# Row blocks woven by two and by four, and an image kept in place, beside a chain of selective scans

## The chip, the cores and the metric

The kernel runs on one core of a Trainium2 chip. What counts is the time of one execution on the device, in microseconds (us). A core has five engines with instruction queues of their own: TensorE (PE; the loading of its weights is shown apart as PEld), VectorE (DVE), ScalarE (ACT), GpSimd (POOL) and SyncE (SP). Here SP issues nearly all DMA transfers, in the order in which they were written down. Each engine takes its instructions strictly in order; an instruction that waits holds up all behind it on the same engine.

## The reference

The input is a batch of four images, each with 96 channels of 64 x 64 pixels (L = 4096). Four layers follow one another, each as x = x + layer(group_norm(x)):

- layer 0: attention of the pixels on pooled queries, and a look at neighbours, then a 5 x 5 depthwise convolution of the values and a projection;
- layer 1: a selective state space layer (`in` projection, 3 x 3 depthwise convolution, scans in four directions over the image, layer norm, a gate), then a block of 1 x 1 (c1), 3 x 3 depthwise (c2) and 1 x 1 (c3) convolutions and a squeeze-and-excitation gate;
- layer 2: a 3 x 3 sharpening filter;
- layer 3: a 1 x 1 convolution with ReLU, a linear layer, and two depthwise branches from it. `x1 = silu(conv(h, dw1))` goes through another selective state space layer. `x2 = silu(conv(h, dw2))` is gated:

```python
x2 = jax.nn.silu(conv2d(h, dw2_w, dw2_b, groups=C))
g = jax.nn.sigmoid(conv2d(jax.nn.relu(conv2d(x2, ag1_w, ag1_b)), ag2_w, ag2_b))
y = x1 + x2 * g
```

The heart of both state space layers is a recurrence along the pixels, `h = h * exp(delta * A) + delta * u * B`, `y = sum over 16 states of h * C`, for 192 channels, 16 states and four directions. For one image and layer these are 12,288 rows of 4096 pixels, or 96 tiles of 128 rows in four chunks of 1024 pixels: 384 units, and eight times that for four images and two layers.

## The kernel before, in words

`streams` (L901) holds everything. Its main loop goes through 3072 units, 384 for each of eight scans (`SCANS`: layer 1 of images 0 and 1, layer 3 of 0 and 1, then the same for 2 and 3). One unit handles 128 rows over a chunk of 1024 pixels:

- SP fetches the step sizes `rep`, four units ahead (L2038);
- ACT takes the exponential, two units ahead (`decays`, L2046), and copies the state at the chunk's end (`carry_on`, L2074);
- PE spreads the inputs into a PSUM tile `bx` (`drive`, two ahead, two such tiles);
- DVE multiplies `bx` by B, one unit ahead (`times_b`, L2059), and runs the recurrence (`scan`, L2066);
- POOL multiplies the result by C (`times_c`, L2078);
- every fourth unit, PE sums states into `acc` (`collect`, 16 matmuls), two to five units behind.

All matmuls have one line, L1028 (`mm`); all weights that are not kept throughout are loaded by `staged` (L991, the transfer named `arena<-in_w`).

Beside the scans runs a generator of side work: `first` (layer 0 and layer 1's `in_conv`), `second` (the rest of layer 1, layer 2, and layer 3 up to its scan), `third` and `last` (the end of layer 3, through `finish`). While scan s goes, `beside(s)` brings other images forward: phases 0, 3 and 4 do `first` of images 1 to 3, phases 1, 2, 5 and 6 `second` of images 0 to 3, and phase 7 `third` three times and `last`. `first` of image 0 runs alone at the start ("the head", to 661 us), and the rest of `last` alone at the end.

The order is written out by hand. A unit gives the side work up to three slots (`Slots.begin` and `end`) against a budget per unit, `PACE`. In the generator, `yield` alone ends the issue of matmuls, whose results the rest of the slot reads; a number ends a step and costs at least half of it; a tuple marks one tap of a convolution, of which as many are taken as the budget holds; `WAIT` uses up the unit's budget. Whatever the generator issues goes into the engines' queues between the scan's own instructions. The preparation of the next group of scans (`prepare`) takes part of most units in the same manner.

PSUM for the side work is two banks, handed out in turn by `bank()`. A step that asks for a bank waits until the last reader of the tile that had it is done. SBUF for the side work is one `arena`, in which `Stack` pools lie on top of each other; a new tile waits for the last users of the bytes under it.

The places that the change touches, by the lines of the kernel before:

- `attention`: keys and queries, a block of 512 pixels at a time: matmul, copy on ACT, square on ACT (L1327), matmul with the heads' ones, maximum on DVE (L1332);
- `first`: weights `l0_*` are staged inside `attention` and again before the 5 x 5 taps; `mix` is the loop of taps, sum, projection and sum (L1491 and L1497); `l1_in` is staged after the second group norm (L1505), right before `in_conv`;
- `second`: c1, c2 and c3 over nine row steps; the squeeze-and-excitation gate (L1619 to L1622); then the residual image is loaded from `res1`, added (L1630), stored to `res1`, loaded once more into a new tile `X`, and normed (L1166 is the norm's first pass on ACT). The norm of layer 3, the 1 x 1 convolution and linear layer (`line`, L1659 and L1664), the gate (L1675 SiLU, L1681 ReLU, L1687 Tanh, L1688 product), x1 (L1699) and `in_conv`;
- `finish`: the gate of the state space layer, SiLU (L1818) and product (L1819).

The gate's rows in `second` are done one after the other, and the last two lines stand in one step:

```python
nc.scalar.activation(q[:96], q[:96], AF.Tanh, bias=half_ag2, scale=0.5)
nc.vector.scalar_tensor_tensor(out=x2, in0=q[:96], scalar=1.0, in1=x2, op0=ALU.add, op1=ALU.mult)
```

Of the kernel before, what the change touches and what calls it, by code (L numbers as in the profile page):

```python
# [9 lines left out]
F32 = mybir.dt.float32  # L10
# [890 lines left out]
def streams(ctx: ExitStack, tc: tile.TileContext, x, wts, cst, out, wat, cat, flag):  # L901
# [42 lines left out]
    class Stack:  # L944
# [14 lines left out]
        def tile(self, shape, dtype, name, tag=None, bufs=None):  # L959
            n = int(np.prod(shape[1:]))  # L960
            tag = tag or name
            if tag not in self.slots:
# [5 lines left out]
                if shape[0] > 96:  # L968
                    self.dirty += [(a, n) for a in self.slots[tag]]
            a = self.slots[tag].pop(0)  # L970
            self.slots[tag].append(a)
            v = arena[: shape[0], a : a + n]
# [252 lines left out]
    def in_conv(pool, tag, b, w, src):  # L1225
# [3 lines left out]
        for h in range(2):  # L1229
# [7 lines left out]
            uc = pool.tile([96, W, H], F32, name="uc", bufs=1)  # L1237
# [69 lines left out]
    def attention(b, xn, samp, dist):  # L1307

        with Stack(2) as pool:
            w = staged(pool, "l0_k", "l0_q", "l0_v")  # L1310
# [14 lines left out]
            def squares(p, o):  # L1325
                sq = pool.tile([96, PCH], F32, tag="sq", name="sq", bufs=1)
# [8 lines left out]
            for j in range(8):  # L1335
                p = bank()
                mm(p[:96], w["l0_k"], xn[:, bass.ts(j, PCH)])
                yield
                nc.scalar.copy(kk[:, bass.ts(j, PCH)], p[:96])
                yield from squares(p[:96], top[:, 0, j : j + 1])  # L1340
            for j in range(2):
# [6 lines left out]
                yield from squares(p[:96], top[:, 1, j : j + 1])  # L1348
            two = small.tile([96, 2], F32, name="two")
# [6 lines left out]
            for pair in [((0, e), (1, e)) for e in range(4)] + [((2, 0), (2, 1)), ((2, 2), (2, 3))]:  # L1356
# [22 lines left out]
                rs = pool.tile([64, Q], F32, tag="sq", name="rs", bufs=1)  # L1379
# [63 lines left out]
    def first(b):  # L1443

        with Stack(1) as P:
            xn = P.tile([96, L], F32, name="xn")
            for j in range(4):
                nc.sync.dma_start(out=xn[:, bass.ts(j, CH)], in_=x[b][:, bass.ts(j, CH)])
            yield from group_norm(xn, img(xn))
            with Stack(1) as D:  # L1450
# [13 lines left out]
                yield from attention(b, xn, samp, dist)  # L1464
                with Stack(1) as FP:
                    feat = FP.tile([96, L], F32, name="feat")
                    yield from neighbours(b, xn, samp, dist, feat)
                    with Stack(1) as pool:
                        w = staged(pool, "l0_v", "l0_proj")
# [11 lines left out]
                        for j in range(8):  # L1481
# [19 lines left out]
            yield from group_norm(xn, img(xn))  # L1501
            for j in range(4):
                nc.sync.dma_start(out=gate1[b][:, bass.ts(j, CH)], in_=xn[:, bass.ts(j, CH)])
            with Stack(1) as pool:
                w = staged(pool, "l1_in")["l1_in"]  # L1505
                yield from in_conv(pool, "l1_", b, w, xn)

    def directions(pool, b, tag):

        V = pool.tile([96, 2, L], F32, name="V", bufs=1)  # L1510
# [29 lines left out]
        return V  # L1540

    def second(b):

        with Stack(1) as PX:
            V = yield from directions(PX, b, "l1_")
# [17 lines left out]
            with Stack(2) as pool:  # L1563
                w = staged(pool, "l1_c1", "l1_c3", "l1_se2")
# [6 lines left out]
                sums = pool.tile([96, 8], F32, name="sums", bufs=1)  # L1571
                for j in range(9):
                    here, last = band[j % 2], band[(j - 1) % 2]
                    if j < 8:
                        for q in range(4):
# [6 lines left out]
                            yield 2  # L1582
                    if j == 0:
# [39 lines left out]
                X = V[:, 1, :]  # L1623
                for j in range(4):
                    nc.sync.dma_start(out=X[:, bass.ts(j, CH)], in_=res1[b][:, bass.ts(j, CH)])
                for j in range(8):
                    js = bass.ts(j, PCH)
                    p = bank()
                    nc.scalar.activation(p[:96], V[:, 0, js], AF.Copy, scale=s2)
                    nc.vector.tensor_add(X[:, js], X[:, js], p[:96])  # L1630
                    nc.sync.dma_start(out=res1[b][:, js], in_=X[:, js])
                    yield 1
        with Stack(1) as R2:
            hp = R2.tile([96, PADW, PADW], F32, name="hp")
            border(hp, 1)
            with Stack(2) as pool:
                X = pool.tile([96, L], F32, name="X", bufs=1)
                for j in range(4):
                    nc.sync.dma_start(out=X[:, bass.ts(j, CH)], in_=res1[b][:, bass.ts(j, CH)])
# [13 lines left out]
                for j in range(8):  # L1653
                    js = bass.ts(j, PCH)
                    p = bank()
                    mm(p[:96], w["l3_c1"], X[:, js])
# [642 lines left out]
```

## Time and profile before

| | |
|---|---|
| time, median of three runs | 13,912.74 us (13,892.47 to 13,918.34) |
| the profiled execution's own time | 13,902.53 us |
| its span, first to last instruction | 13,900.7 us |
| mean granted TensorE clock | 0.899 |
| the scan's loop | 661 to 13,781 us |
| phases begin at | 661, 2268, 3888, 5480, 7080, 8670, 10,258 and 11,848 us |

The page gives, for each engine, its busy time, and below that groups of instructions: line, engine, operation, output <- input, shape and count, then the total of busy time, the mean of one in ns, and the idle time of the engine before them with what ended most of it. "Waits" list for each engine what its instructions waited for: total us, times, and the longest. In a timeline a line is one instruction or several alike: start, duration, engine, line, operation, and in brackets the idle time before it and the releaser. A releaser is worked out from semaphore events, and a matmul's end is modelled, so that a busy PE may still have been slow.

### The profile page before, as it was taken

To read this page: it belongs to the slowest core of one execution; us is meant where nothing else is said; L and a number is where in the kernel's file an instruction comes from. 1 tells how busy PE (TensorE), PEld (TensorE's weight loads), DVE (VectorE), ACT (ScalarE), POOL (GpSimd) and SP (SyncE) were. 2 spreads that over 40 slices of the span, in tenths; PEclk is the share of its full clock that TensorE was granted. 3 is DMA by queue.
4 is the path that set the end of the run, shared out by engine and by line. 5 is a ranking of instruction groups with operands and counts; after the bars stand their busy time and mean duration, and the time that the engine had idled before them with its cause. 6 is when DMAs were issued, how large, how long until landed. Compare 5 with 4: busy or idle time off the path is not lost. (4 is left out here: it accounts for less than half of the span.)

```text
span 13900.7 us, 127815 instructions
## 1 busy us (share of the span) xinstructions
PE 11053.6 (80%) x40137; PEld 3344.3 (24%) x40802; DVE 11634.9 (84%) x7509; ACT 8696.5 (63%) x12314; POOL 10284.9 (74%) x4730
## 2 busy tenths in 40 slices
PE   8878886988779796878868887897969887677756
PEld 3322221322223221222212221232313222111111
DVE  1478988987989888889888898898989988877886
ACT  3366576666756676665766566666856677665654
POOL 1177887877878777788878888787878878666674
PEclk9999998998889897999979998998979998888867
DMA  0267888887878888778877788787888878767774
GB/s 11 64 170 198 202 221 214 204 212 183 230 196 219 212 211 214 187 193 213 221 194 197 196 209 230 192 222 196 224 212 207 222 198 229 183 176 195 184 201 115
DMA packets 846672, 2695.23 MB, mean 194 GB/s; under 512 B 112480, under 2 KB 115008, under 8 KB 845984
## 3 DMA queue, kind: packets, MB, share of 16 engines
q1 hardware_dynamic: 845328, 2685.08, 75.7%
q8 instruction: 324, 5.31, 0.2%
q14 instruction: 364, 2.98, 0.1%
q10 hardware_dynamic: 656, 1.87, 0.0%
HBM read 2186.34 MB, written 500.17 MB: 193 GB/s over the span
## 5 line engine op out<-in xcount | busy, mean ns | idle before, releaser
L2078 POOL TENSOR_TENSOR rep<-hs,bc 128x1024 f32<-128x1024 f32 x3072 | 7226.5, 2359 | 2578.9 <-DVE hs L2066 2189.7
L1028 PE MATMUL one<-arena 128*96 128x512 f32 (+5 forms) x11072 | 5273.9, 602 | 699.8 <-ACT arena L1375 138.0
L2066 DVE TENSOR_TENSOR_SCAN hs<-rep,carry,bx 128x1024 f32<-128x1024 f32 x2304 | 5401.6, 2344 | 296.7 <-ACT carry L2074 25.6
L2059 DVE TENSOR_TENSOR bx<-bx,bc 128x1024 f32<-128x1024 f32 x3072 | 3717.8, 1210 | 666.5 <-PE bx L1028 485.7
L2046 ACT ACTIVATE rep<-rep,l_decay 128x1024 f32<-128x1024 f32 x3072 | 3496.9, 1143 | 799.0 <-DMA rep<-dd 782.4
L1028 PE MATMUL bx<-parts,spread 128*128 128x512 bf16 x5479 | 1879.2, 418 | 1322.8 <-DVE hs L2066 1199.8
L1028 PEld LDWEIGHTS one<-arena 128*96 128x96 f32 (+4 forms) x11072 | 1791.7, 172 | 3128.9 <-issue 1800.3
L2066 DVE TENSOR_TENSOR_SCAN hs<-rep,bx 128x1024 f32<-128x1024 f32 x768 | 1754.4, 2284 | 133.7 <-ACT carry L2074 53.5
L1028 PE MATMUL acc<-rep,ct 128*32 128x512 f32 x12288 | 1712.5, 670 | 12.9 <-POOL rep L2078 9.7
L1028 PEld LDWEIGHTS <-spread 128*128 128x128 bf16 x6144 | 444.6, 100 | 3633.6 <-DVE hs L2066 2362.8
L1028 PE MATMUL one<-pr,ct 64*96 64x512 f32 x1024 | 629.7, 699 | 92.4 <-ACT pr L1953 37.2
L1375 ACT ACTIVATE arena<-one 128x512 f32<-128x512 f32 x576 | 342.3, 595 | 489.8 <-PE one L1028 488.3
L1028 PEld LDWEIGHTS acc<-rep,ct 128*32 128x32 f32 x12288 | 359.1, 118 | 1163.5 <-issue 935.6
L2046 ACT ACT_TABLE_LOAD x482 | 618.4, 1283 | 8.5
L2074 ACT COPY carry<-hs 128x1 f32<-128x1 f32 x2304 | 408.3, 177 | 233.0 <-DVE hs L2066 231.5
L1028 PE MATMUL bx<-arena 128*96 128x512 f32 (+5 forms) x1120 | 489.2, 576 | 34.8 <-DMA arena<-in_w 16.7
L1028 PE MATMUL one<-arena,ct 128*96 128x512 f32 x508 | 294.0, 687 | 249.9 <-ACT arena L1526 177.0
L1028 PE MATMUL held<-arena,cols 128*32 128x256 f32 x3072 | 479.4, 394 | 13.4 <-ACT arena L1375 11.7
L1028 PE MATMUL held<-arena 128*32 128x256 f32 x3072 | 479.9, 394 | 0.0
L982 POOL MEMSET arena<- 32x1024 f32 (+5 forms) x81 | 54.1, 691 | 403.8 <-ACT arena L1375 331.5
L1028 PE MATMUL one<-us,wt 128*38 128x512 f32 x1024 | 284.6, 677 | 72.9 <-DMA us<-urow 36.0
L1988 ACT ACT_TABLE_LOAD x256 | 328.4, 1283 | 4.4
(3322 smaller groups left out, 9857.3 us busy)
## 6 DMA issues: line engine op xcount, KB each, us to landing
rep<-dd SPq DMA_DIRECT2D x3072, 512.0 KB
parts<-du SPq DMA_DIRECT2D x1024, 144.0 KB
bc<-rows SPq DMA_DIRECT2D x256, 512.0 KB
dd<-delta SPq DMA_DIRECT2D x256, 384.0 KB
du<-cut SPq DMA_DIRECT2D x256, 384.0 KB
yrow<-yo SPq DMA_DIRECT2D x128, 512.0 KB
ycol<-yo SPq DMA_DIRECT2D x128, 512.0 KB
us<-urow SPq DMA_DIRECT2D x128, 384.0 KB
```

What stands on the lines that cost most here:

```text
L982: nc.gpsimd.memset(arena[96:, k : min(k + CH, a + n)], 0.0)
L1028: nc.tensor.matmul(o, lhsT=lhsT, rhs=rhs, start=first, stop=last)
L1375: nc.scalar.activation(last.rearrange("p a b -> p (a b)"), p, AF.Exp, scale=HD**-0.5)
L1988: nc.scalar.activation(w, w, AF.Ln)
L2046: nc.scalar.activation(a, a, AF.Exp, scale=decay[tag][:, k, NG * h + m : NG * h + m + 1])
L2059: nc.vector.tensor_mul(bx, bx, ready[i // NG][2][:, 0, :])
L2066: nc.vector.tensor_tensor_scan(out=hs, data0=a, data1=bx, initial=carry[:, h, m : m + 1] if c else 0.0, op0=ALU.mult, op1=ALU.add)
L2074: nc.scalar.copy(carry[:, h, m : m + 1], live[i][1][:, CH - 1 : CH])
L2078: nc.gpsimd.tensor_tensor(a, hs, ready[i // NG][2][:, 1, :], ALU.mult)
```

## The change

A helper `weave(made, depth)` goes round a list of generators; in each pass it takes in one more while fewer than `depth` are active, and runs each up to its next number. Keys and queries, mix and line are passed through it with depth 2, the gate's rows (`skip`) with depth 4. In the gate a step of 0.5 is put between Tanh and product, x2 has five buffers and g1 three, both sets of diagonals are built at the start, and one unit's budget is given up after that. `sq` has four buffers (shared with `ex`) instead of one.

In `second` the residual image X is the second half of V for the rest of the stage. It is loaded from `res1` in row step 7 of c1/c2, and not stored there again; copy and sum of the residual become two half steps. x1 and the turned image of `in_conv` lie in V too.

Weights are staged elsewhere: layer 0's at the start of `first`, `l1_in` ahead of the second group norm, c1, c3 and se2 at the start of `second`; `l3_in` right ahead of `in_conv` instead of ahead of x1's convolutions. In `finish`, a step of 0.5 lies between the gate's SiLU and its product.

```diff
@@ -1222,7 +1222,7 @@
-    def in_conv(pool, tag, b, w, src):
+    def in_conv(pool, tag, b, w, src, turned=None):
@@ -1234,7 +1234,7 @@
                 yield 1
-            uc = pool.tile([96, W, H], F32, name="uc", bufs=1)
+            uc = turned if turned is not None else pool.tile([96, W, H], F32, name="uc", bufs=1)
             for j in range(8):
@@ -1304,10 +1304,26 @@
-    def attention(b, xn, samp, dist):
+    def weave(made, depth):
+
+        left, active = list(made), []
+        while left or active:
+            if left and len(active) < depth:
+                active.append(left.pop(0))
+            for g in list(active):
+                while True:
+                    try:
+                        v = next(g)
+                    except StopIteration:
+                        active.remove(g)
+                        break
+                    yield v
+                    if v is not None and not isinstance(v, tuple):
+                        break
+
+    def attention(b, xn, w, samp, dist):
         with Stack(2) as pool:
-            w = staged(pool, "l0_k", "l0_q", "l0_v")
             kk = pool.tile([96, L], F32, name="kk", bufs=1)
@@ -1332,13 +1348,14 @@
-            for j in range(8):
+            def keys(j):
                 p = bank()
...
                 yield from squares(p[:96], top[:, 0, j : j + 1])
-            for j in range(2):
+
+            def queries(j):
                 p = bank()
@@ -1346,6 +1363,8 @@
                 yield from squares(p[:96], top[:, 1, j : j + 1])
+
+            yield from weave([keys(j) for j in range(8)] + [queries(j) for j in range(2)], 2)
             two = small.tile([96, 2], F32, name="two")
@@ -1446,6 +1465,7 @@
                 nc.sync.dma_start(out=xn[:, bass.ts(j, CH)], in_=x[b][:, bass.ts(j, CH)])
+            w = staged(P, "l0_v", "l0_k", "l0_q", "l0_proj")
             yield from group_norm(xn, img(xn))
@@ -1461,12 +1481,11 @@
                 yield 2
-                yield from attention(b, xn, samp, dist)
+                yield from attention(b, xn, w, samp, dist)
                 with Stack(1) as FP:
...
                     with Stack(1) as pool:
-                        w = staged(pool, "l0_v", "l0_proj")
                         vpad = pool.tile([96, 68, 68], F32, name="vpad")
@@ -1478,7 +1497,7 @@
                             nc.sync.dma_start(out=xn[:, bass.ts(j, CH)], in_=x[b][:, bass.ts(j, CH)])
-                        for j in range(8):
+                        def mix(j):
                             js = bass.ts(j, PCH)
@@ -1498,16 +1517,17 @@
                             yield 1
-            yield from group_norm(xn, img(xn))
-            for j in range(4):
-                nc.sync.dma_start(out=gate1[b][:, bass.ts(j, CH)], in_=xn[:, bass.ts(j, CH)])
+
+                        yield from weave([mix(j) for j in range(8)], 2)
             with Stack(1) as pool:
                 w = staged(pool, "l1_in")["l1_in"]
+                yield from group_norm(xn, img(xn))
+                for j in range(4):
+                    nc.sync.dma_start(out=gate1[b][:, bass.ts(j, CH)], in_=xn[:, bass.ts(j, CH)])
                 yield from in_conv(pool, "l1_", b, w, xn)
-    def directions(pool, b, tag):
-
-        V = pool.tile([96, 2, L], F32, name="V", bufs=1)
+    def directions(V, b, tag):
+
         with Stack(1) as T:
@@ -1537,12 +1557,14 @@
                 yield 1
-        return V
...
         with Stack(1) as PX:
-            V = yield from directions(PX, b, "l1_")
+            V = PX.tile([96, 2, L], F32, name="V", bufs=1)
+            held_w = Stack(1).__enter__()
+            w = staged(held_w, "l1_c1", "l1_c3", "l1_se2")
+            yield from directions(V, b, "l1_")
             with Stack(2) as pool:
@@ -1561,7 +1583,6 @@
             with Stack(2) as pool:
-                w = staged(pool, "l1_c1", "l1_c3", "l1_se2")
                 dg = [diagonals(pool, wv("l1_c2")[:, q, :], f"dg{q}") for q in range(4)]
@@ -1569,6 +1590,7 @@
                 sums = pool.tile([96, 8], F32, name="sums", bufs=1)
+                X = V[:, 1, :]
                 for j in range(9):
@@ -1580,6 +1602,9 @@
                             yield 2
+                    if j == 7:
+                        for k in range(4):
+                            nc.sync.dma_start(out=X[:, bass.ts(k, CH)], in_=res1[b][:, bass.ts(k, CH)])
                     if j == 0:
@@ -1620,23 +1645,17 @@
                 nc.vector.tensor_scalar(s2, s2, 1.0, None, ALU.add)
-                X = V[:, 1, :]
-                for j in range(4):
-                    nc.sync.dma_start(out=X[:, bass.ts(j, CH)], in_=res1[b][:, bass.ts(j, CH)])
                 for j in range(8):
...
                     nc.scalar.activation(p[:96], V[:, 0, js], AF.Copy, scale=s2)
+                    yield 0.5
                     nc.vector.tensor_add(X[:, js], X[:, js], p[:96])
-                    nc.sync.dma_start(out=res1[b][:, js], in_=X[:, js])
-                    yield 1
-        with Stack(1) as R2:
-            hp = R2.tile([96, PADW, PADW], F32, name="hp")
+                    yield 0.5
+            held_w.__exit__()
+            hp = PX.tile([96, PADW, PADW], F32, name="hp")
             border(hp, 1)
             with Stack(2) as pool:
-                X = pool.tile([96, L], F32, name="X", bufs=1)
-                for j in range(4):
-                    nc.sync.dma_start(out=X[:, bass.ts(j, CH)], in_=res1[b][:, bass.ts(j, CH)])
                 pad = pool.tile([96, PADW, PADW], F32, name="pad2", bufs=1)
@@ -1650,10 +1669,10 @@
                 yield from group_norm(X, img(X))
-                for j in range(8):
-                    js = bass.ts(j, PCH)
+
+                def line(j):
                     p = bank()
-                    mm(p[:96], w["l3_c1"], X[:, js])
+                    mm(p[:96], w["l3_c1"], X[:, bass.ts(j, PCH)])
                     yield
@@ -1663,21 +1682,25 @@
                     yield 1
+
+                yield from weave([line(j) for j in range(8)], 2)
             with Stack(2) as pool:
...
                 dg = diagonals(pool, wv("l3_dw2_w"))
-                for j in range(8):
-                    js = bass.ts(j, PCH)
+                dg1 = diagonals(pool, wv("l3_dw1_w"), "diag1")
+                yield WAIT
+
+                def skip(j):
                     p = bank()
                     yield from conv(p[:96], dg, hp, j)
-                    x2 = pool.tile([96, PCH], F32, name="x2")
+                    x2 = pool.tile([96, PCH], F32, name="x2", bufs=5)
                     nc.scalar.activation(x2, p[:96], AF.Silu, bias=wv("l3_dw2_b"))
...
                     yield
-                    g1 = pool.tile([48, PCH], F32, name="g1")
+                    g1 = pool.tile([48, PCH], F32, name="g1", bufs=3)
                     nc.scalar.activation(g1, p[:48], AF.Relu, bias=wv("l3_ag1_b", 48))
@@ -1685,21 +1708,23 @@
                     nc.scalar.activation(q[:96], q[:96], AF.Tanh, bias=half_ag2, scale=0.5)
+                    yield 0.5
                     nc.vector.scalar_tensor_tensor(out=x2, in0=q[:96], scalar=1.0, in1=x2, op0=ALU.add, op1=ALU.mult)
-                    nc.sync.dma_start(out=skip3[b][:, js], in_=x2)
+                    nc.sync.dma_start(out=skip3[b][:, bass.ts(j, PCH)], in_=x2)
                     yield 1
-            with Stack(1) as pool:
-                x1 = pool.tile([96, L], F32, name="x1", bufs=1)
-                dg = diagonals(pool, wv("l3_dw1_w"))
-                w = staged(pool, "l3_in")["l3_in"]
+
+                yield from weave([skip(j) for j in range(8)], 4)
+                x1 = V[:, 0, :]
                 for j in range(8):
...
                     p = bank()
-                    yield from conv(p[:96], dg, hp, j)
+                    yield from conv(p[:96], dg1, hp, j)
                     nc.scalar.activation(x1[:, js], p[:96], AF.Silu, bias=wv("l3_dw1_b"))
...
                     yield 1
-                yield from in_conv(pool, "l3_", b, w, x1)
+            with Stack(1) as pool:
+                w = staged(pool, "l3_in")["l3_in"]
+                yield from in_conv(pool, "l3_", b, w, x1, V[:, 1, :].rearrange("p (a b) -> p a b", b=H))
@@ -1715,7 +1740,8 @@
         with Stack(1) as PX:
-            V = yield from directions(PX, b, "l3_")
+            V = PX.tile([96, 2, L], F32, name="V", bufs=1)
+            yield from directions(V, b, "l3_")
             yield from finish(PX, b, V, [(0, range(8))])
@@ -1816,6 +1842,7 @@
                         nc.scalar.activation(p[:96], p[:96], AF.Silu)
+                        yield 0.5
                         nc.vector.scalar_tensor_tensor(out=V[:, h, js], in0=V[:, h, js],
```

Not shown: the list of regions that a pool clears holds each only once and takes in every tile over 96 partitions; a name or two in signatures.

More of the change, by code (lines that the diff above doesn't have):

```diff
@@ L967, in tile @@
                 assert mark[0] <= ARENA, mark[0]
-                if shape[0] > 96:
-                    self.dirty += [(a, n) for a in self.slots[tag]]
             a = self.slots[tag].pop(0)
             self.slots[tag].append(a)
+            if shape[0] > 96 and (a, n) not in self.dirty:
+                self.dirty.append((a, n))
             v = arena[: shape[0], a : a + n]
@@ L1325, in squares @@
             def squares(p, o):
-                sq = pool.tile([96, PCH], F32, tag="sq", name="sq", bufs=1)
+                sq = pool.tile([96, PCH], F32, tag="ex", name="sq", bufs=4)
                 nc.scalar.activation(sq, p, AF.Square)
@@ L1378, in attention @@
                 yield
-                rs = pool.tile([64, Q], F32, tag="sq", name="rs", bufs=1)
+                rs = pool.tile([64, Q], F32, name="rs", bufs=1)
                 nc.vector.reciprocal(rs, av[:64, :Q])
```

## The prediction

> **What bounds the kernel now.** I read the page's busy shares first, then the groups of the scan's line, then the windows of one phase, and last the waits of DVE, PE and ACT over the loop (661 to 13,781 us).
>
> The page, span and busy shares:
>
> ```profile
> span 13900.7 us, 127815 instructions
> PE 11053.6 (80%) x40137; PEld 3344.3 (24%) x40802; DVE 11634.9 (84%) x7509; ACT 8696.5 (63%) x12314; POOL 10284.9 (74%) x4730
> ...
> L2066 DVE TENSOR_TENSOR_SCAN hs<-rep,carry,bx 128x1024 f32<-128x1024 f32 x2304 | 5401.6, 2344 | 296.7 <-ACT carry L2074 25.6
> L2059 DVE TENSOR_TENSOR bx<-bx,bc 128x1024 f32<-128x1024 f32 x3072 | 3717.8, 1210 | 666.5 <-PE bx L1028 485.7
> ```
>
> DVE is the fullest engine, and it sets the time as a chain: each of 3072 units does one scan (2.34 us) and one product (1.21 us). By the scans' start times a unit with nothing else on DVE takes 3.60 us. 3072 of these are 11,060 us; the loop takes 13,119 us. Some 2,060 us are therefore excess, which the side work causes: DVE instructions of its own, or waits that it puts in DVE's queue or ahead of PE's `bx` matmuls. Only that can change. The side work of all phases but the eighth is done 30 to 47 units before its phase ends, so that spreading it over more units costs nothing by itself.
>
> Waits of DVE in the loop (total us, times, longest):
>
> ```profile
> DVE bx L2059 <- PE bx L1028: 485.7, 263, 17.2
> DVE arena L1688 <- ACT one L1687: 94.2, 30, 5.8
> ...
> DVE arena L1332 <- PE one L1028: 48.2, 21, 4.5
> ...
> DVE arena L1819 <- ACT one L1818: 33.6, 29, 2.7
> ...
> DVE arena L1630 <- DMA arena<-res: 11.9, 5, 7.9
> ```
>
> The second line is layer 3's gate: the product with the tanh (L1688) stands at once behind Tanh's order, and Tanh behind a matmul; a scan queued behind it waits too. The first collects what holds PE up; PE's and ACT's own waits say what:
>
> ```profile
> PE one L1028 <- DMA arena<-in_w: 67.4, 12, 10.4
> ...
> PE one L1028 <- ACT arena L1681: 39.3, 30, 3.1
> ```
>
> ```profile
> ACT arena L1166 <- DMA arena<-res: 32.8, 3, 11.3
> ...
> ACT arena L1166 <- DMA arena<-in_w: 12.3, 1, 12.3
> ```
>
> A matmul waits up to 10.4 us for staged weights, with the `bx` matmuls queued behind it; ACT waits four times, 45.1 us, for the image that `second` has just stored and loads again (the fourth is filed under in_w, but its line reads that image).
>
> **The change part by part.** All against the profiled execution: span 13,900.7 plus 1.8 around it, 13,902.5 us. It is 10.2 below the median of 13,912.7, inside the runs' 13,892 to 13,918.
>
> *1. Weave by two (keys and queries, mix, line): 0.* `weave` adds one generator per pass and each row yields a number twice. So row 1 begins only after row 0's second number: the issue order stays k0, h0, k1, h1. In the changed program's instruction streams the order is the same as before on PE up to the second stage's pooled vectors, and on DVE through all of phase 0. `sq` with four buffers instead of one moves nothing while the order stays. L1332's 48.2 us remain.
>
> *2. Layer 3's gate by four: -84.* Rows have four numbers now, so here the order does change: the convolution of row j+1 and the other rows' steps come between Tanh and product, and the product follows by a round. By the scans, the 32 units that hold the gate's rows take 155.4, 153.8, 149.8 and 148.6 us in the four images; quiet they would take 115.3. Excess together 146.4. Of it stays DVE's own 32 products x 0.686 = 22; the neighbouring stage (x1's eight convolutions, no waits) has an excess of 3.5 in 24 units, 0.15 per unit, so 34 units x 4 = 20; and PE still waits for ReLU (L1681 39.3, here only as far as no row lies between): I leave 20. 146 - 62 = 84. Bounds: 50 if the ReLU and SiLU waits (39.3 and L1675's 28.8, about half on the path) come on top; 124 if only the products stay. PE is a ceiling near: 130 us busy in such a stretch of 150.
>
> ```profile
> 9606.00:9756.00 150.00, 129.48 (x391) 39.01 (x398) 116.23 (x72) 102.41 (x140) 100.59 (x44) 0.93 0.68 171
> ...
> 3391.00:3485.00 94.00, 91.77 (x302) 31.23 (x306) 87.24 (x52) 72.02 (x82) 79.34 (x35) 0.99 0.83 221
> ```
>
> These windows (length; PE, PEld, DVE, ACT, POOL busy; clock; DMA) show the gate's stretch and x1's: there PE is 98% busy, and DVE still goes at 3.7 us per unit. The second set of diagonals puts two POOL instructions of 1.63 us back to back ahead of `times_c`; POOL is 100 of 150 busy there, and `collect` stands two units behind: 0.
>
> *3. The image in place: -39.* Gone are eight stores and four loads per image and the waits for them: at the norm's start the units have an excess of 13.4, 8.7, 8.1 and 8.5 = 38.7. The read of `res1` moves to row 7 of c1/c2: its last part waits on SP for PE's last reader, and the `rep` loads queued behind it run four units (14 us) ahead, so it is hidden; without that cover it would cost one c1 step, about 5. Bounds -43 and -30.
>
> *4. Residual: -8.* L1630 no longer waits for the image (11.9). Its copy and sum are split by a half slot; the sum may come later, never earlier. Bounds 0 and -18.
>
> *5. Weights earlier.* `l1_in` before the norm: PE gaps of 9.5, 10.4, 10.4 and excesses of 6.0, 8.3, 8.4 in these units (three images; the first's is in the head), against 1.9 where the same convolution starts without a wait: -17 (-10 to -23). Layer 0's weights and c1's at their stage's start: PE gaps of 8.3, 7.4, 7.8 and 1.5, 3.3, 3.3, and 5.5 where layer 2's weights stood in SP's queue behind the image's loads, 37 in all. `l1_in`'s gaps cost 17 of 30; these are shorter, and two `bx` buffers cover more of a short one, so I take 40%: -15 (-30 to 0). In the head the first value matmul at 40.3 waits 16.7 for weights, while `xn` is ready at 32.9: -7 (-8 to -3).
>
> *6. `l3_in` later: +23.* Today it is staged 24 convolutions before its use; now at the start of `in_conv`, with the first matmul in the same slot. Nearest row, the same form for `l1_in`:
>
> ```profile
> 1878.32 0.43 SPq L991 DMA_DIRECT2D arena<-in_w  x1
> ...
> 1883.23 1.99 PE L1028 MATMUL one<-arena 128*96 128x512 f32 x2 [9.51 <-DMA arena<-in_w]
> ...
> 1886.12 1.23 DVE L2059 TENSOR_TENSOR bx<-bx,bc 128x1024 f32<-128x1024 f32 x1 [5.88 <-PE bx L1028]
> ```
>
> Issue to matmul is 4.91 us; on PE it costs 9.51 because SP's order, the drive of the next unit and DVE all stand behind. 4 x (7.6 - 1.9) = +23; bounds +15 and +34.
>
> *7. Gates of the finish: 0 (-20 to +31).* A half slot between SiLU (L1818) and product (L1819). The same generator goes on, so no other side work comes between, and DVE's order stays; the next unit's Exp can come between. That makes 24 more table loads on ACT (14 for SiLU, 10 for Exp):
>
> ```profile
> 12007.66 1.28 ACT L2046 ACT_TABLE_LOAD   x1
> 12008.96 1.15 ACT L2046 ACTIVATE rep<-rep,l_decay 128x1024 f32<-128x1024 f32 x1
> ```
>
> 24 x 1.28 = 31 us of an ACT that is 63% busy, beside DVE; on the path at worst all of it. Against that stand 33.6 us that L1819 waits now, of which some may go.
>
> This is where a rule speaks against the change. The Trainium skill (ScalarE: Activation LUTs, "What ACT_TABLE_LOAD costs") puts a switch at 2.66 us, since it adds a drain of 1.38 to the load; by that the 24 switches would be 64 us and the bound +64. The rows above show no such gap: Exp starts 1.30 us after the load's start.
>
> Sum: -84 - 39 - 8 - 17 - 15 - 7 + 23 = -147, giving 13,902.5 - 147 = 13,755.5. A shift of where the later stages fall against the scan's groups is worth about 20 either way (line's excess in the four images is 19.5, 14.2, 15.0, 12.4).
>
> **The rivals.**
> - *The gate's wait changes its name.* A row's PSUM bank `q` is held from Tanh until its product, a round later, so everything else has one bank: each convolution waits for the ReLU before. For: PE already waits there 30 times, 1.3 on average. Against: half of PE's waits were hidden elsewhere. The gate then gives 30 instead of 84: 13,810.
> - *The table loads lie on the path:* +31, 13,787. For: the fence above lies in this stage, where ACT goes back and forth between the two tables already. Against: ACT's 63%.
> - *More is freed:* the finish's 33.6 and 30 more in the gate (its upper bound with the shift): 13,692.
> - *Weave by two interleaves after all:* most of 48.2 goes, 13,715. The order speaks against it.
> - *Slower:* the same held bank stalls PE so long that DVE starves in the gate. It decides from (147 + 28)/32 = 5.5 us per row on the path. Today's longest wait of PE there is 5.7 (for L1659, one step earlier); at 5.7 each, 32 x 5.7 = +182: 13,938.
>
> **How the numbers follow.** No change is taken as within 0.2%, 28 us, about what the runs can tell. The sum's case 60% (13,710 to 13,800); the gate's wait renamed 13%, a quarter of which with the other gains also missing, so within 0.2%; table loads 10%; more freed 9%; weave by two 2%; slower 6%. Faster 0.91, same 0.03, slower 0.06. The range takes in all but the slower case and the extremes: 13,680 to 13,850.
>
> **What would show it.** Right: L1712's (now the product) waits for Tanh under 25 us; no ACT wait at L1166 for the image; the gate's four stretches near 137 us in 34 units; a new PE wait of about 9 us for weights at the start of layer 3's `in_conv`, and none at layer 1's. Step 1 is right if keys' reduction still waits about 48. Wrong: PE waits for ReLU (now L1704) growing beyond 60, or DVE waiting for `bx` longer than today's 485.7 in spite of the weights.

## The result, and the profile after

The changed kernel takes 13,759.4 us (median of four runs, 13,736 to 13,771); the kernel before, in the same runs, 13,915.5. The ratio is 0.9893, with a 95% interval of 0.9881 to 0.9906: 1.07% faster. The forecast was 13,755, with 13,680 to 13,850 as its range. The profiled execution took 13,771.1 us, the slowest of the four, 131 less than the profiled one before.

The page of the changed kernel, span and busy shares:

```profile
span 13769.2 us, 128385 instructions
...
PE 11150.4 (81%) x40802; PEld 3349.2 (24%) x40802; DVE 11633.7 (84%) x7509; ACT 8718.5 (63%) x12338; POOL 10280.4 (75%) x4730
```

DVE does the same work in the same time (11,633.7 us against 11,634.9): all of the gain is waiting that has gone. Waits of DVE in the changed kernel's loop, 648 to 13,647 us (total us, times, longest):

```profile
DVE bx L2086 <- PE bx L1028: 647.4, 389, 14.4
...
DVE arena L1348 <- PE one L1028: 44.0, 21, 3.0
...
DVE arena L1846 <- ACT one L1844: 28.6, 30, 2.7
```

The wait of the product for Tanh (94.2 before) is gone from the list, and so is the residual's wait for its image. The keys' reduction (44.0) waits as it did. `bx` must be read with care: 665 records of `bx` matmuls are missing from the trace before, so that there the wait is filed under four releasers. From the loop's start to the end, before:

```profile
DVE bx L2059 <- PE bx L1028: 485.7, 263, 17.2
...
DVE bx L2059 <- PE one L1028: 66.9, 60, 6.1
DVE bx L2059 <- PE acc L1028: 64.0, 47, 11.4
...
DVE bx L2059 <- remote: 44.8, 8, 30.0
```

and after:

```profile
DVE bx L2086 <- PE bx L1028: 677.9, 390, 30.5
...
DVE bx L2086 <- DMA rep<-dd: 1.2, 2, 1.0
```

Together that was 661 us and is 679. So the waits for `bx` did not shrink, although much that held PE up has gone. That is the first sign that something took its place.

Waits of PE there:

```profile
PE one L1028 <- ACT arena L1704: 25.8, 18, 3.1
PE one L1028 <- DMA arena<-in_w: 25.1, 4, 6.9
...
PE one L1028 <- DVE arena L1712: 20.4, 16, 1.9
```

The first line is the gate's ReLU (39.3 before). The last is new: a matmul waits for the product, the last reader of the PSUM bank that it is to write. Of the waits for weights (67.4 in 12 before) four are left, and all four are new: layer 3's `in` weights. One of them in the timeline:

```profile
5014.03 0.58 SPq L991 DMA_DIRECT2D arena<-in_w  x1
...
5019.59 3.58 PE L1028 MATMUL one<-arena 128*96 128x512 f32 x4 [6.86 <-DMA arena<-in_w]
...
5023.64 1.23 DVE L2086 TENSOR_TENSOR bx<-bx,bc 128x1024 f32<-128x1024 f32 x1 [6.83 <-PE bx L1028]
```

From issue to matmul it takes 5.6 us; 6.86 us of waiting on PE become 6.83 us on DVE.

For the rest I use one measure. From each scan's start to the next, less the 3.604 us of a quiet unit, is the unit's excess; summed over the units that a stage occupies and over the four images, it tells what the stage costs. The changed kernel was profiled twice (the second time as the reference of a later job), which shows how far this measure is steady:

| stage, excess in us | before | changed | changed, again |
|---|---|---|---|
| head (start of the loop) | 661.5 | 647.7 | 645.8 |
| `first`: attention | 297.6 | 285.3 | 279.8 |
| `first`: values, taps, mix | 85.4 | 77.6 | 75.8 |
| `first`: layer 1's `in_conv` | 103.4 | 82.2 | 85.9 |
| `second`: squeeze-and-excitation, residual | 36.9 | 19.5 | 19.4 |
| `second`: first norm of the image | 64.5 | 20.0 | 20.1 |
| `second`: line | 58.5 | 42.5 | 41.2 |
| `second`: gate | 151.3 | 84.8 | 81.6 |
| `second`: x1 | 27.8 | 13.6 | 12.4 |
| `second`: layer 3's `in_conv`, to the phase's end | 120.5 | 176.0 | 168.1 |
| all units of the loop | 2049.1 | 1929.0 | 1890.2 |

The stages that were to gain did, by about what was forecast or more, and the gate by less (67 to 70 against 84). But `in_conv` of layer 3 lost 48 to 55 us, where 23 were expected.

### The profile page after: what moved, and what is told of

Same layout as the page of the kernel before. It is cut to its first block, busy times and chain, and to the rows that moved or that the text cites. A ratio compares the mean times of both kernels' runs of the same rounds, so it can differ in the third digit from the quotient of the medians.

```text
span 13769.2 us, 128385 instructions
## 1 busy us (share of the span) xinstructions
PE 11150.4 (81%) x40802; PEld 3349.2 (24%) x40802; DVE 11633.7 (84%) x7509; ACT 8718.5 (63%) x12338; POOL 10280.4 (75%) x4730
## 5 line engine op out<-in xcount | busy, mean ns | idle before, releaser
L1028 PE MATMUL bx<-parts,spread 128*128 128x512 bf16 x6144 | 2030.3, 415 | 1338.7 <-DVE hs L2093 1225.9
```

Of the source, the lines that this page charges most:

```text
L1028: nc.tensor.matmul(o, lhsT=lhsT, rhs=rhs, start=first, stop=last)
```

## The experiments

The kernel before takes 13,887 to 13,916 us by the job, so kernels of different jobs are compared by their ratio to the one before in the same job. The changed kernel's is 0.9893 and, in the second job, 0.9897; I take 0.9895. Each ratio's interval is 0.0013 to 0.0017 either way, some 20 us, and a difference between two kernels is less sure than either. The scans' units go in groups of twelve; while one group runs, the next is prepared.

**Layer 3's `in` weights early.**

```diff
+            w3 = staged(PX, "l3_in")["l3_in"]
             with Stack(2) as pool:
                 w = staged(pool, "l3_ag2")
...
             with Stack(1) as pool:
-                w = staged(pool, "l3_in")["l3_in"]
-                yield from in_conv(pool, "l3_", b, w, x1, V[:, 1, :].rearrange("p (a b) -> p a b", b=H))
+                yield from in_conv(pool, "l3_", b, w3, x1, V[:, 1, :].rearrange("p (a b) -> p a b", b=H))
```

> The changed kernel with one edit: layer 3's `in` weights are staged before the gate's rows, so that they lie there long before `in_conv`. Reference for all: the changed kernel's 13,759 us. Theory (the prediction's step 6, with its size from the trace after): the wait for them and the two units after it that catch up cost 12 us in each of four images, 2 of them in any case: -40, 13,719; by the prediction's own size -23, 13,736. Rival (only the place against the scan's groups of twelve units counts, and the wait is hidden): 0, 13,759, and `in_conv` keeps its excess of about 34 us in each image.

Measured: 13,737.4, ratio 0.9888 (0.9872 to 0.9905), 10 us under the changed kernel's and not distinguishable from it. In the trace no matmul waits for weights any more. The first nine units of `in_conv` have an excess of 23.9, against 46.8 and 46.1 in the changed kernel: 22 less, the prediction's own size for this step. The other 51 units of its work stay at 84.3, where they had 59.7 before and 90.0 and 84.3 in the changed kernel. So the wait is worth 22 by the trace; the timing shows 10, with 20 either way. The second half of `in_conv`'s loss is something else.

**The gate's rows one after another.**

```diff
                     nc.scalar.activation(q[:96], q[:96], AF.Tanh, bias=half_ag2, scale=0.5)
-                    yield 0.5
                     nc.vector.scalar_tensor_tensor(out=x2, in0=q[:96], scalar=1.0, in1=x2, op0=ALU.add, op1=ALU.mult)
...
-                yield from weave([skip(j) for j in range(8)], 4)
+                yield from weave([skip(j) for j in range(8)], 1)
```

> The changed kernel with the gate's rows one after another again, Tanh and product in one step. Theory (step 2): the gate's stretch gets back its waits for Tanh, about 90 us, and its excess grows from 73 to about 146 over four images: +73, 13,832; by the prediction's size +84, 13,843. Rival (the wait only changes its name, and most of the gain is from stages moving to other places): +30, 13,790.

Measured: 13,737.1, ratio 0.9886 (0.9869 to 0.9902): 12 us under the changed kernel, inside the interval. The weave by four is undone, and nothing is lost; the rival's 13,790 is missed too, on the other side. The gate's excess rises as expected in kind (121.5 against 81.6 and 84.8), but only by 38, and `in_conv` falls from 168 to 176 down to 122.7. From the gate's begin to the phase's end the four images have 265.8 here, and 285.2 and 272.9 with the weave.

**The image loaded twice again.**

```diff
-                    if j == 7:
-                        for k in range(4):
-                            nc.sync.dma_start(out=X[:, bass.ts(k, CH)], in_=res1[b][:, bass.ts(k, CH)])
...
                 nc.vector.tensor_scalar(s2, s2, 1.0, None, ALU.add)
+                for j in range(4):
+                    nc.sync.dma_start(out=X[:, bass.ts(j, CH)], in_=res1[b][:, bass.ts(j, CH)])
...
                     nc.vector.tensor_add(X[:, js], X[:, js], p[:96])
+                    nc.sync.dma_start(out=res1[b][:, js], in_=X[:, js])
...
             border(hp, 1)
             with Stack(2) as pool:
+                for j in range(4):
+                    nc.sync.dma_start(out=X[:, bass.ts(j, CH)], in_=res1[b][:, bass.ts(j, CH)])
```

> The changed kernel with the residual image loaded after the squeeze-and-excitation gate, stored to `res1` and loaded again before the norm, as before. Theory (steps 3 and 4): the norm waits for the image again, +44 in four images, and the residual sum for its load, +8 to +18: together 13,811 to 13,821. Rival (the stages behind take up the wait, since the side work has room in its phase): below +15, 13,760 to 13,774.

Measured: 13,810.5, ratio 0.9940 (0.9923 to 0.9956): +0.0045, 62 us. The norm's excess is 63.0 again (20.0 without), the residual's only 24.6 (19.5; 36.9 before), with the half step between copy and sum left in. ACT's wait is back in the trace of this run:

```profile
ACT arena L1166 <- DMA arena<-res: 40.1, 4, 10.7
```

**A weave by two that alternates.** `weave` takes in as many rows as the depth allows at once, where the depth is two; the gate keeps its order.

```diff
-            if left and len(active) < depth:
+            while left and len(active) < depth:
                 active.append(left.pop(0))
+                if depth > 2:
+                    break
```

> The changed kernel with a weave by two that takes in both rows at once, so that keys and queries, mix and line really alternate; the gate's weave by four as it is. Theory (step 1: by two the order did not change): the order changes now, and the 44 us for which DVE waits in the keys' reduction shrink, as do the ReLU waits in line: -20 to -45, 13,714 to 13,739. Rival (the alternation was there already, or the wait moves to the two PSUM banks): 0, 13,759.

Measured: 13,657.9, ratio 0.9829 (0.9812 to 0.9845): -0.0066, 92 us faster than the changed kernel, twice the best that I had expected. The order was indeed not changed before. DVE's waits of this run, for the keys' maximum and for mix's projection (44.0 and 32.5 in the changed kernel):

```profile
DVE arena L1350 <- PE one L1028: 16.6, 13, 4.0
...
DVE arena L1518 <- PE one L1028: 3.6, 4, 1.5
```

By stages: line 42 to 8.7, taps and mix 77 to 43.0, attention 283 to 249.3: some 100 together, less 5 to 7 by which the loop starts later. I had left mix out of the expectation's sum.

**The changed kernel again**, as the reference of the second job.

> The changed kernel once more, as a reference beside the next three on one chip. All theories: 0.9893 of the time of the kernel before on this chip, inside its interval (0.988 to 0.991).

Measured: 13,749.8, ratio 0.9897 (0.9880 to 0.9914). Its profiled span is 13,728.6, against 13,769.2 in the other profile of the same program.

**`in_conv` moved by nine units.**

```diff
             with Stack(1) as pool:
+                for _ in range(9):
+                    yield WAIT
                 w = staged(pool, "l3_in")["l3_in"]
```

> The changed kernel with nine units of pause ahead of layer 3's `in_conv`, so that it begins at unit 296 of its phase instead of 287. With the gate's rows one after another it began at 284, which is the same place in the groups of twelve units; there its excess was 123 us over four images, against 176 in the changed kernel. Theory (the place against the groups, at which the next group is prepared, decides: the gate's weave gained some 40 us in its own stretch and moved `in_conv` by three units into a worse place): in_conv's excess falls to about 125, so -50 against the changed kernel in the same job. Rival (the weave leaves something behind, such as tiles in the arena that `in_conv` has to wait for): the excess stays near 176, and the time is unchanged within 15.

Measured: 13,748.4, ratio 0.9892 (0.9875 to 0.9908), -1 us against the reference. By time the theory fails, and the rival's two numbers hold (an excess of 164 against 168, the time unchanged); its reason, something that the weave leaves behind, is not shown. By stages the loss moves: the 51 units after `in_conv`'s start fall from 84.3 to 55.0 at the other place, but its first nine rise from 46.1 to 55.5, and the units behind it, to the phase's end, from 37.7 to 53.6. So the place decides how much is lost where, and the loss as a whole was not reduced. The place was not all that changed, though: PE's wait for the weights, which are still staged late here, grew from 24.6 to 40.5 us.

**The finish without its half step.**

```diff
                         nc.scalar.activation(p[:96], p[:96], AF.Silu)
-                        yield 0.5
```

> The changed kernel without the half step between SiLU and product in the gates of `finish`. The prediction's step 7: 0, between -31 (if the 24 table loads that the step brings lay on the path) and +20. Theory: table loads fall from 52 to 38 at that line and from 492 to about 482 for Exp, DVE's waits for the SiLU rise from 29 to about 34, and the time against the changed kernel in the same job stays within 10.

Measured: 13,757.7, ratio 0.9899 (0.9882 to 0.9915), 8 us over the reference: no difference that these runs can tell. ACT's table loads in the changed kernel:

```profile
L2073 ACT ACT_TABLE_LOAD x492 | 631.2, 1283 | 8.8
...
L1844 ACT ACT_TABLE_LOAD x52 | 66.7, 1283 | 0.9
```

and without the half step:

```profile
L2072 ACT ACT_TABLE_LOAD x476 | 610.7, 1283 | 8.3
...
L1844 ACT ACT_TABLE_LOAD x38 | 48.8, 1283 | 2.5 <-PE one L1028 1.9
```

30 loads, 38.5 us of ACT, cost the whole nothing that can be seen, and DVE waits 5.7 us less with them (28.6 against 34.3).

**Weights staged where they were.** Layer 0's, `l1_in` and those of c1, c3 and the squeeze-and-excitation gate; layer 3's as changed.

```diff
-            w = staged(P, "l0_v", "l0_k", "l0_q", "l0_proj")
...
         with Stack(2) as pool:
+            w = staged(pool, "l0_k", "l0_q", "l0_v")
...
                     with Stack(1) as pool:
+                        w = staged(pool, "l0_v", "l0_proj")
                         vpad = pool.tile([96, 68, 68], F32, name="vpad")
...
-                w = staged(pool, "l1_in")["l1_in"]
                 yield from group_norm(xn, img(xn))
                 for j in range(4):
                     nc.sync.dma_start(out=gate1[b][:, bass.ts(j, CH)], in_=xn[:, bass.ts(j, CH)])
+                w = staged(pool, "l1_in")["l1_in"]
...
-            held_w = Stack(1).__enter__()
-            w = staged(held_w, "l1_c1", "l1_c3", "l1_se2")
...
             with Stack(2) as pool:
+                w = staged(pool, "l1_c1", "l1_c3", "l1_se2")
```

> The changed kernel with layer 0's weights, `l1_in` and the weights of c1, c3 and the squeeze-and-excitation gate staged where they were before; the rest as changed. Theory (step 5 and the head): PE waits for weights again, 8 to 10 us at a time, and by the prediction the time rises by 17 + 15 + 7 = 39 against the changed kernel in the same job; by the stretches of the two traces `in_conv` of layer 1 gives 21 of it, the values' matmuls 9 and the head 14. Rival (only the place of stages counts, which this does not move): under 15.

Measured: 13,800.9, ratio 0.9931 (0.9914 to 0.9947), +51 us against the reference. PE's waits for weights in this run:

```profile
PE one L1028 <- DMA arena<-in_w: 95.8, 16, 10.8
```

(24.6 in 4 in the reference). The loop starts at 658.2 instead of 645.8, attention has 303.6 instead of 279.8 (285.3 in the other profile), layer 1's `in_conv` 101.2 instead of 85.9, the taps 84.5 instead of 75.8: 60 together. The head, `in_conv` and the taps were expected; the largest share, 24 in attention, was not.

**Both gains together.**

> The changed kernel with both edits that helped: the weave by two that really alternates, and layer 3's `in` weights staged ahead of the gate. As a ratio to the kernel before in the same job: the first alone gave 0.983, the second 0.989 against the changed kernel's 0.9893 to 0.9897, with its stretch 22 us shorter in the trace. Theory (the two add up): 0.9813 to 0.983, about 13,640. Rival (the second's gain is taken back by the place of the stages behind): 0.983.

Measured: 13,641.7, ratio 0.9812 (0.9798 to 0.9825). They add up.

**The same with the gate's rows one after another.** The edit is that of the second experiment.

> As the run before, with the gate's rows one after another, Tanh and product in one step: the weave by four tested a second time, now with both others in place and in one job. Theory (from the first such run: the weave gains 40 us in its own stretch and costs as much in `in_conv`, which begins three units later and is slower there): within 15 us of the run before. Rival (the first such run was chance, the weave is worth its own stretch): 35 to 45 us slower than the run before.

Measured: 13,626.7, ratio 0.9801 (0.9787 to 0.9814), 15 us faster than with the weave, with intervals that overlap. The gate's excess is 128.4 (87.2 with it), `in_conv`'s 84.9 (144.6 with it). DVE's wait for `bx` from the loop's start to the end, with the weave:

```profile
DVE bx L2088 <- PE bx L1028: 594.9, 371, 29.8
```

and without it, where the product waits for Tanh again:

```profile
DVE bx L2087 <- PE bx L1028: 531.9, 324, 30.0
...
DVE arena L1714 <- ACT one L1713: 65.8, 28, 4.3
```

594.9 against 531.9 + 65.8 = 597.7, in one profile of each. What the weave takes from Tanh comes back as waiting for PE's `bx`, and it comes back there: from the gate's begin to the phase's end DVE waits 134.7 us for `bx` with the weave and 70.8 without. Of these 64 us 29 lie in the gate and x1, 35 behind them.

**The gate's rows woven by two**, both taken in at once.

> As the first of these runs, with the gate's rows woven by two instead of by four, both rows taken in at once. `in_conv` begins at unit 287 as there. Theory (one other row between Tanh and product is enough to hide Tanh, and the place behind is the same): within 15 us of the first. Rival (two rows leave half of the Tanh waits): 15 to 30 us slower.

Measured: 13,633.6, ratio 0.9805 (0.9791 to 0.9818), between the last two. The gate's excess is the lowest of all, 56.2; x1 has 25.5 instead of 14.3 and `in_conv` 146.4. The gate's own stretch can be made 72 us shorter than with rows, and the kernel is no faster for it.

**The gate wholly as before.**

```diff
-                dg1 = diagonals(pool, wv("l3_dw1_w"), "diag1")
-                yield WAIT
...
-                    x2 = pool.tile([96, PCH], F32, name="x2", bufs=5)
+                    x2 = pool.tile([96, PCH], F32, name="x2")
...
-                    g1 = pool.tile([48, PCH], F32, name="g1", bufs=3)
+                    g1 = pool.tile([48, PCH], F32, name="g1")
...
+                dg1 = diagonals(pool, wv("l3_dw1_w"), "diag1")
                 x1 = V[:, 0, :]
```

with depth one and without the half step, as in the second experiment.

> The changed kernel with the whole gate as before: rows one after another, x2 and g1 with two buffers each, and x1's diagonals built after the gate. In the run with the rows one after another alone, the stretch still had 30 us less excess than before (121 against 151) and x1's 17 less. Theory (these 47 us are a matter of where the gate begins in the groups of twelve, unit 226 instead of 222 or 223): unchanged against that run, a ratio of 0.989 to the kernel before. Rival (the buffers and the early diagonals brought them): 0.992, some 45 us slower.

Measured: 13,792.0, ratio 0.9922 (0.9908 to 0.9935): +0.0036, 50 us over the rows alone, and +38 over the changed kernel. The rival's number holds, the theory's does not. DVE's wait for Tanh in this run:

```profile
DVE arena L1709 <- ACT one L1708: 111.8, 32, 6.3
```

and with the rows alone, early diagonals and more buffers kept:

```profile
DVE arena L1711 <- ACT one L1710: 67.2, 29, 5.2
```

45 us less of the same wait. The early diagonals show in PE's waits for them: here

```profile
PE one L1028 <- POOL arena L1200: 9.4, 8, 2.2
```

and with the rows alone:

```profile
PE one L1028 <- POOL arena L1200: 1.3, 4, 0.3
```

Which of the edits does the rest (the buffers of x2 and g1, the diagonals, or the unit given up after them) was not tried apart. The place is not excluded as a cause: the unit given up moves all that follows, and `in_conv` has 143.5 here instead of 122.7, with 33.7 instead of 4.7 in one unit alone (unit 313 of the phase, over the four images).

## Why the prediction was right, and where it was wrong

The number was right within 5 us, and that closeness is luck: errors cancel. The gate was taken as worth too much, the image and the weights too little, the late `l3_in` as too dear.

- *Bound.* Right: DVE's busy time did not move, and the gain is its waits alone.
- *Step 1, weave by two, 0.* Right, and tested: keys still wait (48.2 before, 44.0 after), and a weave that does alternate is 92 us faster. Line's excess fell by 16 all the same, with its order unchanged; its place in the groups of units changed, which was allowed 20 either way; that the place did it is not shown.
- *Step 2, the gate, -84.* Wrong, and the step that failed. The mechanism was seen correctly in its own stretch (no wait for Tanh, excess 151 to 83, so -68; of the 62 that the sum left in the stretch, 83 are there). But what a stage loses less is not what the kernel gains. Undone as a whole, the gate's edits cost 38 us; with the weave alone undone, the kernel was 12 and 15 us faster in the two experiments, so the gain of the gate's edits lies in the early diagonals, the buffers and the unit given up, not in the weave. x1 gained 14 us that no term of the sum had. The first rival named this, a wait that changes its name, but put it on the next convolution's wait for ReLU. PE's waits for ReLU fell instead (39.3 to 25.8), and the held bank showed as 20.4 us of waiting for the product. The wait came back at DVE's `bx`, half of it in the gate and x1, half in `in_conv` behind them. Of the prediction's own signs of being wrong, this one came: DVE waits longer for `bx` (647.4 us against 485.7, or 679 against 661 with all releasers counted). The prediction had the warning in its own windows, that PE is 130 us busy in a stretch of 150 and 98% in the next, and used it as a ceiling for one stage only.
- *Steps 3 and 4, the image, -47.* Right in kind. Undone, 62 us (0.9940 against 0.9895, each with 20 either way). By stages the norm gave 44 and the residual 17, for which the sum had 39 and 8: the residual is at its bound of 18. Undone, the residual lost only 5 of its 17 again, so most of that is not the wait for the image; whether it is the half step, to which the prediction gave nothing, no run shows.
- *Step 5 and the head, -39.* Right in kind, somewhat more: 51 when undone. The head gave 14 to 16 against 7, outside its bounds of 3 to 8; I had bounded it by when the norm's output is ready for one matmul, and did not look for others behind it. `l1_in` gave 17 to 21 against 17.
- *Step 6, `l3_in` late, +23.* Right in place and size: a new wait of 6.3 us per image on PE (25.1 in four, 6.9 at most; the prediction had about 9), 22 us of excess by the trace when it is taken away. In the timing 10 of it show, inside the interval.
- *Step 7, the finish, 0.* Right within what can be told: 8 us the other way when undone. The lower price of a table load, or none at all, holds: 30 loads more, of 38.5 us of ACT, are hidden. In the changed kernel's trace the next instruction of ACT starts 1.29 us after a load's start (median of 1018). The Trainium skill (ScalarE: Activation LUTs, "What ACT_TABLE_LOAD costs") has 2.66 us for each, which would make an estimated 80 us of ACT; the drain that it adds does not show in this trace, and no run here shows a cost of these loads.
- *The shift of places, 20 either way.* Too small for `in_conv` of layer 3: besides the 22 us of its wait it lost another 26 to 33, and the run that moved it by nine units showed 29 us moving out of its convolutions and 25 coming back before and behind them.

The runs, by what each part is worth when undone: gate 38, image 62, weights and head 51, finish about 8, against -10 for `l3_in`: 149 together. The measured change is 156 by the medians (13,915.5 less 13,759.4). For the first three the sum had 84, 47 and 39, and for the last two 0 and -23. Each of the five has some 20 us either way, so that 149 and 156 agree within what the runs can tell.

What stays open: why `in_conv` loses with a weave ahead of it. That it begins three units later is not the whole of it. The place, tried at nine units' distance, moved the loss but did not remove it. The two kernels with the alternating weave by two show where PE's time goes. Over 60 units from `in_conv`'s start, in all four images, with 2888 and 2891 matmuls, PE is busy for 882 us with the weave by four and 859 without, and idle for 94 and 49; the mean granted clock is 0.962 and 0.991. Part of the idle time is PE waiting for ACT: from `in_conv`'s start to the phase's end it waits 28.0 us for `in_conv`'s copies and 16.3 for the exponential in the next group's preparation, against 8.7 and 4.6 without the weave; for the preparation's own copies it waits 7.3 against 15.0. Why the order of the gate's rows leads to that, and whether the lower clock adds to the loss or only goes with it, no run here shows.

The fastest kernel of these runs is the one with the alternating weave by two, layer 3's weights early and the gate's rows one after another: 13,626.7 us, a ratio of 0.9801 (0.9787 to 0.9814) to the kernel before, 1% under the changed kernel. It keeps the early diagonals and the buffers of the change.

## What to carry to other kernels

When hand-placed side work runs beside a chain that one engine sets, and a second engine is nearly full as well, a stall that is taken out of one stage can come back in the next as waiting for that second engine: count a stage's gain only after adding the stages behind it, up to the point where the schedule has slack. Undo an edit alone before giving it credit; here the weave that gave the change its name was worth nothing, and its helper's smaller use was a no-op that taking in both rows at once (`while` for `if`) turned into 92 us. A load that is issued in the slot of its first use can cost its latency on the engines queued behind that use (here 5.6 us from issue to matmul, and 6.9 us of waiting on PE and 6.8 on DVE), and is cheap to move.

## What the runs showed of the hardware that was not expected

Two profiled executions of the same program had spans of 13,769.2 and 13,728.6 us, 0.3% apart, with the excess of single stages differing by 8 us (neighbours 90.7 and 82.4, `in_conv` of layer 3 176.0 and 168.1). One profile against another says nothing of 40 us in the whole; the norm (20.0 and 20.1) and the gate (84.8 and 81.6) are much steadier.
